# Row numbers of a neighbour search: added by a second product, or written into PSUM by ScalarE ahead of one product

## The chip, the cores and the metric

The kernel runs on one core of a Trainium2 chip. The metric is the device time of one execution in microseconds (us). A run is timed three times and the median is given. A separate execution is recorded by the profiler.

The engines are called by the profile's names: PE (TensorE), DVE (VectorE), ACT (ScalarE), POOL (GpSimd), SP (SyncE). Each works through its own queue in order. The matrix products write into PSUM[...].

## The reference

There are 4096 nodes of 128 features and an adjacency matrix of 4096 x 4096 integers, of which about one in 128 is 1. Cut to what matters:

```python
# layer 0: attention over the neighbours, 8 heads
Wh  = einsum('nd,hde->hne', nodes, W)
e   = leaky_relu(f1[:, :, None] + f2[:, None, :], 0.2)      # f1 = Wh.a1, f2 = Wh.a2
att = softmax(where(adj > 0, e, -9e15), axis=-1)
h   = elu(einsum('hnm,hmd->hnd', att, Wh))
x   = layernorm(nodes + elu(cat(h) @ W1 + b1))
# layer 1: for each node three quantiles over its kept neighbours, feature by feature
keep  = mask & ~((rank + 1) % skip == 0)
svals = sort(where(keep[:, :, None], x[None], big), axis=1)
agg   = mean of svals at ceil(q * n_keep) - 1, q in (0.25, 0.5, 0.75)
out   = (0.5 * agg + 0.5 * x) @ W.T + b + x
```

The kernel never forms the dense arrays: it finds each node's list of neighbours, at most 64, and gathers their rows.

## The kernel before, in words

**Three blocks.** The 32 tiles of 128 nodes are treated in blocks of 6, 10 and 16 (`BLOCKS`). For each block there is a *search* for the lists and then *attention*. The search of block 0 runs alone, beside the setup of the node rows (`node_rows`). Afterwards the attention of block 0 runs beside the search of the 10 tiles, and the attention of the 10 tiles beside the search of the 16. The prediction calls these two stretches block 0 and block 1. The attention of the last 16 tiles runs beside the making of layer 1's lists. Then comes the sort of layer 1, mostly on DVE.

**The search** (`neighbours`, L627). `load` (L634) brings half a tile of the adjacency matrix in a DMA of 1 MB, issued from ACT's queue; `sign` (L641) turns it into bfloat16 marks 0 or 1 (sgn) on ACT, sums them into cnt and issues the next load. A half tile has four chunks of 512 columns. For each chunk two products into one PSUM bank form keys: L684 multiplies the marks by 8192, and L687 adds a number that falls with the column (4096 minus the column), from two rows of `parts`. Thus a neighbour's key is over 8192 and tells its column. `eights` (L649) takes the eight largest of each 128 columns, four maxima a chunk (L651); `best` (L653) takes the eight largest that are left of the tile before (L656) and blanks them (L658). After eight chunks a tile is done; after up to four tiles `complete_records` writes them as records. The keys have two banks (pool kp), so the product of one chunk waits for the maxima of two chunks before. One chunk with its best is a *piece* of the generator, and the search yields after each.

**A step of attention** (`step`, L371). `fetch_rows` (L912) queues a tile's gathers on POOL, one indirect DMA for each slot of the list (L219), into tiles G of 16 slots. There are six G. `attend` (L938) works on the tile fetched one step earlier: the scores z (DVE, then an exponential on ACT, L959), their sums den on PE (L967) into the bank `small`, the reciprocals rden (DVE), spread by PE into rz (L983), multiplied into z (L994), laid out as wide (L1002), and then the weighted sums y on PE (L1015), one product for each slot with its G as weights. Only when these are done is a G free for the gathers of a later tile. The step's second half is done in the next step beside the next tile's first half: y is copied by ACT to yT (named late, L1028), PE multiplies with W into hT (L1034), ACT and DVE form the elu hv (L1040, L1042, L1043), PE multiplies with W1 into o (L1046), in the bank `small` too, and `finish_x1` makes the layer-0 row: v (L1069), ve, and rstd (L1081), scattered by POOL (L228).

**The order.** Within a step both generators are advanced in turn, and pieces of the search are put between them by count (`quota`). All of PE, DVE, ACT and POOL keep the order in which the program is written out (`manual_schedule`); only SP's is left to a scheduler. At the end of a block the search is finished, `rank_by_count` orders the block's nodes by list length, and POOL scatters the records among the last tile's gathers; SP reads them back as R and narrow.

**PSUM banks:** two for keys, one `small`, one rz, two y, two hT.

Of the kernel before, what the change touches and what calls it, by code (L numbers as in the profile page):

```python
# [9 lines left out]
F32 = mybir.dt.float32  # L10
BF16 = mybir.dt.bfloat16
I32 = mybir.dt.int32
AF = mybir.ActivationFunctionType
ALU = mybir.AluOpType
AX = mybir.AxisListType
PSUM = bass.MemoryType.PSUM
# [3 lines left out]
P = 128  # L20
N = 4096
D = 128
H = 8
# [6 lines left out]
L = 64  # L30
# [2 lines left out]
MARK = 8192.0  # L33
ROUNDS = L // 8
GROUP = 4
STEPS = 24
KEEP_MIN = 6.0
FMAX = 30.0
# [197 lines left out]
def iota(nc, dst, pattern, base=0, cm=0):  # L236
    nc.gpsimd.iota(  # L237
        dst, pattern=pattern, base=base, channel_multiplier=cm, allow_small_or_imprecise_dtypes=True
    )
# [3 lines left out]
def kernel(  # L243
# [15 lines left out]
    nc = tc.nc  # L259

    dram = ctx.enter_context(tc.tile_pool(name="dram", bufs=1, space=DRAM))
    xt_d = dram.tile([N + P, XW], F32, name="xt_d")
# [7 lines left out]
    ident = const.tile([P, P], F32, name="ident")  # L270
# [5 lines left out]
    pidx = const.tile([P, 1], F32, name="pidx")  # L276
    jp1 = const.tile([P, L], F32, name="jp1")
    vecs = const.tile([P, 4, D], F32, name="vecs")
    W_sb = const.tile([P, H, D], F32, name="W_sb")
    W1_sb = const.tile([P, H, D], F32, name="W1_sb")  # L280
    wa = const.tile([P, 2 * H], F32, name="wa")
    WlT = const.tile([P, D], F32, name="WlT")
    total = const.tile([1, 1], I32, name="total")
    bad = const.tile([P, 5, NT], F32, name="bad")
# [4 lines left out]
    rec = rp.tile([P, NT, REC], F32, name="rec")  # L289
    num = rp.tile([P, NT], F32, name="num")  # L290
    oneb = rp.tile([P, P], BF16, name="oneb")
    before = rp.tile([P, P], BF16, name="before")
    adjp = tc.alloc_tile_pool(name="adjp", bufs=2, side="right")
    cp = tc.alloc_tile_pool(name="cnt", bufs=2, side="right")
    kp = tc.alloc_tile_pool(name="key_ps", bufs=2, space=PSUM)
    parts = [adjp.tile([64, n], BF16, name=f"parts{n}", bufs=1) for n in (N // 8, 7 * N // 8)]
    markb = adjp.tile([P, P], BF16, name="markb", bufs=1)
    rowi = adjp.tile([P, P], F32, name="rowi", bufs=1)

    def search(t0, n):  # L300
        return neighbours(
            tc, adjp, cp, kp, rec, num, adj, t0, n, parts, markb, oneb, bad, jp1, pidx
        )

    with tc.tile_pool(name="setup", bufs=1) as sp, tc.tile_pool(
        name="setup_ps", bufs=2, space=PSUM
    ) as pp, tc.manual_schedule(engines=ORDERED):

        for v in parts:
            nc.vector.memset(v, 0.0)  # L310
        nc.vector.memset(oneb, 1.0)
        for v, base in zip(parts, (N, N - N // 8)):
            n = v.shape[1] // 64
            iota(nc, v[0:1, :], [[-64, n], [0, 64]], base=base)
            iota(nc, v[32:33, :], [[0, n], [-1, 64]])
        nc.vector.tensor_scalar(markb, ident, MARK, None, ALU.mult)
        iota(nc, pidx, [[0, 1]], cm=1)
        iota(nc, jp1, [[1, L]], base=1)
        nc.gpsimd.iota(
            rec.bitcast(I32)[:, :, R_OWN], pattern=[[P, NT]], base=0, channel_multiplier=1  # L320
        )
        iota(nc, rowi, [[1, P]])
        rows = node_rows(tc, sp, pp, rec, x, W, W_sb, a1, a2, Wl, wa, WlT, ident, bad, xt_d)
        for i, _ in enumerate(search(0, BLOCKS[0])):
            if i > 0:
                next(rows, None)
        for _ in rows:
            pass
        nc.vector.tensor_scalar(before, rowi, pidx, None, ALU.is_gt)
        nc.sync.dma_start(W1_sb, W1.rearrange("(h e) o -> e h o", e=P))  # L330
        for i, v in enumerate((b1, gamma, beta, bl)):
            nc.sync.dma_start(vecs[:, i, :], v.partition_broadcast(P))
        for i, big in enumerate((-BIG, BIG)):
            fill = sp.tile([P, D], F32, name=f"fill{i}")
            nc.gpsimd.memset(fill, big)
            nc.sync.dma_start(x1_d[N + i * P : N + (i + 1) * P, :], fill)
    attp = tc.alloc_tile_pool(name="att", bufs=2, reuse_waits="tile")
    pp = tc.alloc_tile_pool(name="att_ps", bufs=1, space=PSUM)
# [3 lines left out]

    weigh, store, tail = [], [], []
    consts = {}
    consts["small"] = pp.tile([P, 512], F32, name="small")

    narrow = {
        w: attp.tile([P, 32 // w, NARROW[w]], F32, name=f"narrow{w}", bufs=1) for w in NARROW
# [62 lines left out]
    t0 = 0  # L411
    with tc.manual_schedule(engines=ORDERED):
# [5 lines left out]
        for w in (32, 16, 8, 4):  # L418
            k = P // w
            v = const.tile([P, k], F32, name=f"v{w}")  # L420
# [7 lines left out]
        for w in (32, 16, 8, 4):  # L428
            k = P // w // 4
            v = const.tile([4, k, P], F32, name=f"vT{w}")  # L430
# [5 lines left out]
            W_sb=W_sb, W1_sb=W1_sb, vecs=vecs, eps_t=eps_t, ident=ident, own=own, ownT=ownT  # L436
        )
        for b, n in enumerate(BLOCKS):
            last = b == len(BLOCKS) - 1
            if last:  # L440
# [5 lines left out]
                cp = tc.alloc_tile_pool(name="cnt_all", bufs=2, side="right", reuse_waits="tile")  # L446
# [51 lines left out]
    with tc.tile_pool(name="sort", bufs=2) as sp, tc.tile_pool(name="fin", bufs=3) as fp, tc.tile_pool(  # L498
        name="fin_ps", bufs=2, space=PSUM
# [124 lines left out]
    return ROUNDS * (n + 1) + 3 * len(groups_of(n))  # L624


def neighbours(tc, adjp, cp, kp, rec, num, adj, t0, n, parts, markb, oneb, bad, jp1, pidx):  # L627


    nc = tc.nc  # L630
    half = N // 2
    loads, signs, firsts = [], [], []

    def load():  # L634
        if todo:
            t, i, cnt = todo.pop(0)
            adj_t = adjp.tile([P, half], I32, name="adj_t", bufs=3)
            nc.scalar.dma_start(adj_t, adj[ts(t, P), ts(i, half)])
            loads.append((t, i, cnt, adj_t))

    def sign():  # L641
        if loads:
            t, i, cnt, adj_t = loads.pop(0)
            sgn = adjp.tile([P, half], BF16, name="sgn", bufs=2)
            nc.scalar.activation(sgn, adj_t, AF.Sign, accum_out=cnt[:, i : i + 1])  # L645
            signs.append(sgn)
            load()

    def eights(key, first, c0):  # L649
        for c in range(512 // CW):  # L650
            nc.vector.max(first[:, ts(c0 // CW + c, 8)], key[:, ts(c, CW)])  # L651

    def best(first, t, r):  # L653

        top, rest = rec[:, t, ts(r, 8)], first[:, 8 * r :]
        nc.vector.max(top, rest)  # L656
        if r < ROUNDS - 1:
            nc.vector.match_replace(rest, top, rest, 0.0)  # L658

    todo, counts = [], {}  # L660
    for t in range(t0, t0 + n):
        cnt = adjp.tile([P, 2], F32, name="cnt", bufs=20)
        todo += [(t, 0, cnt), (t, 1, cnt)]
        counts[t] = cnt
    for _ in range(3):
        load()
    sign()
    late = None
    start = t0
    for t in range(t0, t0 + n + 1):  # L670

        if t < t0 + n:
            first = adjp.tile([P, NCH * 8], F32, name="first")
            firsts.append(first)
        for r in range(ROUNDS):
            done = late
            late = None
            if t < t0 + n:
                b = r % (ROUNDS // 2)
                if b == 0:  # L680
                    sgn = signs.pop(0)

                key = kp.tile([P, 512], F32, name="key")
                nc.tensor.matmul(  # L684
                    key, lhsT=markb, rhs=sgn[:, ts(b, 512)], start=True, stop=False
                )
                nc.tensor.matmul(  # L687
                    key, lhsT=oneb[0:64, :], rhs=parts[1][:, ts(r - 1, 512)] if r else parts[0], start=False, stop=True
                )
                late = (key, first, r * 512)  # L690
                if b == 0:
                    sign()
            if done:
                eights(*done)
            if t > t0:
                best(firsts[-2 if t < t0 + n else -1], t - 1, r)
            yield
        if t > t0:
            u = t - 1
            cnt = counts[u]  # L700
            nc.vector.tensor_tensor(num[:, u : u + 1], cnt[:, 0:1], cnt[:, 1:2], ALU.add)
            nc.vector.tensor_scalar(rec[:, u, 0:L], rec[:, u, 0:L], -MARK, 0.0, ALU.add, ALU.max)
            if t - t0 in groups_of(n):
                yield from complete_records(tc, cp, rec, num, bad, jp1, pidx, start, t - start)
                start = t
# [232 lines left out]
def attend(tc, ap, pp, fetched, consts):  # L938


    nc = tc.nc
    R, mine, parts = fetched
# [16 lines left out]
    nc.scalar.activation(zs, zs, AF.Exp)  # L959
    yield  # L960

    small = consts["small"]
    den = small[:, 0 : 32 * H]
    for i, (w, g0, runs, f1v) in enumerate(parts):
        k = P // w
        for r in range(k // 4):
            nc.tensor.matmul(  # L967
                den[0:4, :].rearrange("p (g r h) -> p r g h", r=k // 4, h=H)[:, r, g0:],
                lhsT=own[w][:, ts(r, 4)],
                rhs=z[:, layer[i] : layer[i] + w - g0, :],  # L970
                start=(i == 0 and r == 0),
                stop=(i == len(parts) - 1),
                skip_group_check=True,
# [2 lines left out]
    rden = ap.tile([4, 32 * H], F32, name="rden", bufs=1)  # L976
    nc.vector.tensor_scalar(rden, den[0:4, :], TINY, None, ALU.max)
    nc.vector.reciprocal(rden, rden)  # L978
    rz = pp.tile([P, L * H], F32, name="rz")
    for i, (w, g0, runs, f1v) in enumerate(parts):  # L980
        k = P // w
        for r in range(k // 4):
            nc.tensor.matmul(  # L983
                rz[:, layer[i] * H : (layer[i] + w - g0) * H],
                lhsT=ownT[w][:, r, :],
                rhs=rden.rearrange("p (g r h) -> p r g h", r=k // 4, h=H)[:, r, g0:],
                start=(i == 0 and r == 0),
                stop=(r == k // 4 - 1),
                skip_group_check=True,
# [51 lines left out]
    yield  # L1041
    nc.vector.tensor_scalar(hf, hf, 1.0, -1.0, ALU.min, ALU.add)  # L1042
    nc.vector.tensor_tensor(hf, hT, hf, ALU.max)  # L1043
    o = small[:, 32 * H : 32 * H + D]
    for h in range(H):
        nc.tensor.matmul(  # L1046
            o, lhsT=hv[:, h, :], rhs=consts["W1_sb"][:, h, :], start=(h == 0), stop=(h == H - 1)
# [453 lines left out]
```

## Time and profile before

| | |
|---|---|
| median of 3 runs | 3558.73 us (3556.36 to 3559.92) |
| the profiled execution's own time | 3561.78 us |
| its span, first to last instruction | 3560.0 us |
| PE busy | 1257.6 us (35%), 5323 products |
| DVE busy | 2700.2 us (76%) |
| ACT busy | 403.2 us (11%), 579 instructions |
| POOL busy | 2510.0 us (71%) |
| key products L684 and L687 | 256 each, 588 and 580 ns in the mean |
| gathers of the attention, L219 into G | 1124, 974 ns in the mean |
| granted clock of PE, mean | 0.562 |

A row of the profile names the line and engine, then what is written and what is read (out<-in), the count, the busy time and the mean of one. A wait names the instruction that ended it. Where the engine named had long been done, it was another. The busy time of products is modelled from a pipelined engine, so the distance from one start to the next says more than the length of one. The share of an engine over the whole span is a mean over stages that are bound by different things.

### The profile page before, as it was taken

How to read it: one execution, taken by the hardware profiler on the slowest of the kernel's cores; microseconds unless marked ns; L12 is line 12 of the kernel's file. 1: busy time of each engine (PE TensorE's matmuls, PEld its weight loads, DVE VectorE, ACT ScalarE, POOL GpSimd, SP SyncE). 2: the span in 40 equal slices, each digit the busy share in tenths (PEclk: the TensorE clock that was granted, in tenths of full speed). 3: DMA queues.
4: the chain of work that ended last, by engine and by line, in shares of the span. 5: the costliest groups of instructions: out<-in, count | busy, mean ns of one | idle time of the engine just before them, and what ended most of it. 6: DMA issues, size and time to landing. Idle time of an engine off the chain costs nothing. (4 is left out here: it accounts for less than half of the span.)

```text
span 3560.0 us, 22296 instructions
## 1 busy us (share of the span) xinstructions
PE 1257.6 (35%) x5323; PEld 949.8 (27%) x5323; DVE 2700.2 (76%) x7015; ACT 403.2 (11%) x579; POOL 2510.0 (71%) x2341
## 2 busy tenths in 40 slices
PE   7377568878555454555620000000000000000101
PEld 2144545555455454454520000000000000000101
DVE  8787458877435222247538999999999999999998
ACT  3122122222111111111110000000000000000000
POOL 1475767657777777777747777788777688777771
PEclk9955556555556555555555555555555555555555
DMA  6442254432222222232211111111111111111110
GB/s 232 136 150 77 67 159 131 139 119 75 59 65 54 56 53 55 54 70 55 52 30 48 47 46 46 43 43 41 44 42 46 34 40 41 41 42 41 40 42 12
DMA packets 109132, 237.42 MB, mean 67 GB/s; under 512 B 46720, under 2 KB 63104, under 8 KB 100800
## 3 DMA queue, kind: packets, MB, share of 16 engines
q0 software_dynamic: 74368, 156.34, 17.6%
q10 hardware_dynamic: 14848, 70.85, 5.8%
q1 hardware_dynamic: 19776, 8.73, 1.2%
q8 instruction: 44, 0.72, 0.1%
q14 instruction: 96, 0.79, 0.1%
HBM read 224.60 MB, written 11.15 MB: 66 GB/s over the span
## 5 line engine op out<-in xcount | busy, mean ns | idle before, releaser
L219 POOL DMA_INDIRECT vals<-x_d,idx x1024 | 1219.8, 1191 | 315.7 <-issue 308.7
L219 POOL DMA_INDIRECT G<-xt_d,idx x1124 | 1094.5, 974 | 419.9 <-issue 330.8
L1228 DVE TENSOR_TENSOR work<-work 128x512 f32<-128x512 f32 (+7 forms) x1194 | 933.7, 811 | 0.6
L1247 PE MATMUL st_ps<-dg,goal 128*128 128x128 f32 x286 | 71.4, 427 | 1605.9 <-DVE goal L1228 1605.1
L1228 DVE TENSOR_TENSOR work<-work,work 128x512 f32<-128x512 f32 (+6 forms) x821 | 590.8, 741 | 0.5
L1015 PE MATMUL y<-wide,G 128*128 128x32 f32 (+3 forms) x2248 | 485.6, 394 | 29.0 <-DVE wide L1002 28.9
L1247 PEld LDWEIGHTS st_ps<-dg,goal 128*128 128x128 f32 x286 | 63.3, 322 | 1612.3 <-issue 1611.4
L1015 PEld LDWEIGHTS y<-wide,G 128*128 128x128 f32 x2248 | 463.5, 310 | 65.4 <-DVE wide L1002 31.8
L651 DVE MAX8 first<-key 128x8 f32<-128x128 f32 x1024 | 225.2, 282 | 109.0 <-PE key L687 108.6
L952 DVE TENSOR_TENSOR z<-G,f1x 128x128 f32<-128x128 f32 (+5 forms) x92 | 28.8, 327 | 307.7 <-DMA G<-xt_d,idx 302.3
L684 PE MATMUL key<-sgn,markb 128*128 128x512 bf16 x256 | 150.5, 588 | 131.8 <-DVE first L651 87.9
L1228 DVE TENSOR_TENSOR work<-vals 128x1536 f32<-128x1536 f32 (+7 forms) x96 | 133.4, 1404 | 47.9 <-DMA vals<-x_d,idx 47.5
L1199 DVE COPY junk<-still 128x1 f32<-128x1 f32 x1118 | 168.8, 151 | 0.0
L645 ACT ACTIVATE sgn<-adj_t 128x2048 bf16<-128x2048 int32 x64 | 122.1, 1907 | 333.8 <-PE key L684 277.9
L1046 PE MATMUL small<-W_sb,late 128*128 128x128 f32 x512 | 127.3, 434 | 88.3 <-DVE late L1043 88.3
L1246 ACT ACTIVATE dg<-ident,wt 128x128 f32<-128x128 f32 x143 | 47.5, 394 | 930.9 <-PE st_ps L1247 930.6
L967 PE MATMUL small<-z,own 128*4 128x32 f32 (+6 forms) x438 | 49.3, 279 | 285.4 <-ACT z L959 285.4
L687 PE MATMUL key<-parts,oneb 64*128 64x512 bf16 x256 | 148.4, 580 | 0.5 <-POOL parts L237 0.5
L1046 PEld LDWEIGHTS small<-W_sb,late 128*128 128x128 f32 x512 | 112.8, 327 | 102.6 <-DVE late L1043 98.9
L983 PE MATMUL rz<-rden,ownT 4*128 4x32 f32 (+6 forms) x438 | 96.6, 383 | 78.6 <-DVE rden L978 63.7
L1034 PE MATMUL hT<-late,W_sb 128*128 128x128 f32 x512 | 110.2, 383 | 35.4 <-ACT late L1028 35.4
L228 POOL DMA_INDIRECT out_dram<-o,own_i x32 | 44.7, 1398 | 105.9 <-ACT o L1273 83.6
(184 smaller groups left out, 1784.4 us busy)
## 6 DMA issues: line engine op xcount, KB each, us to landing
adj_t<-in_adj_dram ACTq DMA_DIRECT2D x64, 1024.0 KB
G<-xt_d,idx POOLq DMA_INDIRECT x1124
vals<-x_d,idx POOLq DMA_INDIRECT x1024
R<-rec_d SPq DMA_DIRECT2D x128, 26.2 KB
xt_d<-rec SPq DMA_DIRECT2D x4, 544.0 KB
rec<-in_x_dram ACTq DMA_DIRECT2D x4, 512.0 KB
narrow<-rec_d SPq DMA_DIRECT2D x68, 5.2 KB
a_b<-in_L_gnn_a_dram ACTq DMA_DIRECT2D x2, 512.0 KB
```

Of the source, the lines that this page charges most:

```text
L219: nc.gpsimd.indirect_dma_start(out=dst, out_offset=None, in_=rows, in_offset=bass.IndirectOffsetOnAxis(ap=idx, axis=0),)
L645: nc.scalar.activation(sgn, adj_t, AF.Sign, accum_out=cnt[:, i : i + 1])
L651: nc.vector.max(first[:, ts(c0 // CW + c, 8)], key[:, ts(c, CW)])
L684: nc.tensor.matmul(key, lhsT=markb, rhs=sgn[:, ts(b, 512)], start=True, stop=False)
L687: nc.tensor.matmul(key, lhsT=oneb[0:64, :], rhs=parts[1][:, ts(r - 1, 512)] if r else parts[0], start=False, stop=True)
L983: nc.tensor.matmul(rz[:, layer[i] * H : (layer[i] + w - g0) * H], lhsT=ownT[w][:, r, :], rhs=rden.rearrange("p (g r h) -> p r g h", r=k // ...
L1015: nc.tensor.matmul(yf[:, ts(g, c)], lhsT=G[:, col + j - a, 0:D], rhs=pf[:, ts(j, c)], start=(i == 0 and g % (w // 2) == w // 2 - 1), stop= ...
L1034: nc.tensor.matmul(hT[:, ts(h, P)], lhsT=consts["W_sb"][:, h, :], rhs=yT[:, h, :], start=True, stop=True)
L1046: nc.tensor.matmul(o, lhsT=hv[:, h, :], rhs=consts["W1_sb"][:, h, :], start=(h == 0), stop=(h == H - 1))
L1199: nc.vector.tensor_copy(junk, late["still"])
L1228: nc.vector.tensor_tensor(slots_of(dst, (j, c, s, m), size), slots_of(a, (i, c, s, m), size), slots_of(b, (i + d, c, s, m), size), op,)
L1247: nc.tensor.matmul(st_ps[:, u, :], lhsT=goal[:, (j * k + u) * D : (j * k + u + 1) * D], rhs=dg, start=(j == 0), stop=False,)
```

## The change

ACT writes a chunk's row numbers into the PSUM bank with one instruction, an Identity of the fixed tile `rows` (0 to -511) plus a bias for each chunk (`base`); PE's one product then adds the marks to what lies there. These writes are called seeds here. The keys have three banks; two seeds are written at the start of a search and each further one two chunks ahead. For each of the three banks an opening product is issued first in each search. The sums den and the output o have no bank of their own any more: den lies in rz, o in hT.

```diff
+KEYS = 3
-    kp = tc.alloc_tile_pool(name="key_ps", bufs=2, space=PSUM)
-    parts = [adjp.tile([64, n], BF16, name=f"parts{n}", bufs=1) for n in (N // 8, 7 * N // 8)]
+    kp = tc.alloc_tile_pool(name="key_ps", bufs=3, space=PSUM)
+    rows = adjp.tile([P, 512], F32, name="rows", bufs=1)
+    base = adjp.tile([P, ROUNDS], F32, name="base", bufs=1)
...
-        for v in parts:
-            nc.vector.memset(v, 0.0)
         nc.vector.memset(oneb, 1.0)
-        for v, base in zip(parts, (N, N - N // 8)):
-            n = v.shape[1] // 64
-            iota(nc, v[0:1, :], [[-64, n], [0, 64]], base=base)
-            iota(nc, v[32:33, :], [[0, n], [-1, 64]])
+        iota(nc, rows, [[-1, 512]])
+        iota(nc, base, [[-512, ROUNDS]], base=N)
...
-    consts["small"] = pp.tile([P, 512], F32, name="small")
...
+    def seed(r):
+
+        key = kp.tile([P, 512], F32, name="key")
+        if len(opened) < KEYS:
+            nc.tensor.matmul(key, lhsT=markb, rhs=signs[0][:, 0:512], start=True, stop=True)
+            opened.append(key)
+        nc.scalar.activation(key, rows, AF.Identity, bias=base[:, r : r + 1])
+        seeded.append(key)
+
     for _ in range(3):
         load()
     sign()
+    opened, seeded = [], []
+    chunks = [r for _ in range(n) for r in range(ROUNDS)]
+    for _ in range(KEYS - 1):
+        seed(chunks.pop(0))
...
-                key = kp.tile([P, 512], F32, name="key")
+                key = seeded.pop(0)
                 nc.tensor.matmul(
-                    key, lhsT=markb, rhs=sgn[:, ts(b, 512)], start=True, stop=False
-                )
-                nc.tensor.matmul(
-                    key, lhsT=oneb[0:64, :], rhs=parts[1][:, ts(r - 1, 512)] if r else parts[0], start=False, stop=True
+                    key,
+                    lhsT=markb,
+                    rhs=sgn[:, ts(b, 512)],
+                    start=False,
+                    stop=True,
+                    skip_group_check=True,
                 )
...
             if done:
                 eights(*done)
+            if chunks:
+                seed(chunks.pop(0))
             if t > t0:
                 best(firsts[-2 if t < t0 + n else -1], t - 1, r)
...
-    small = consts["small"]
-    den = small[:, 0 : 32 * H]
+    rz = pp.tile([P, L * H], F32, name="rz")
+    den = rz[:, 0 : 32 * H]
...
-    rz = pp.tile([P, L * H], F32, name="rz")
...
-    o = small[:, 32 * H : 32 * H + D]
+    o = hT[:, 0:D]
```

More of the change, by code (lines that the diff above doesn't have):

```diff
@@ L301, in search @@
         return neighbours(
-            tc, adjp, cp, kp, rec, num, adj, t0, n, parts, markb, oneb, bad, jp1, pidx
+            tc, adjp, cp, kp, rec, num, adj, t0, n, rows, base, markb, bad, jp1, pidx
         )
@@ L322 @@
         iota(nc, rowi, [[1, P]])
-        rows = node_rows(tc, sp, pp, rec, x, W, W_sb, a1, a2, Wl, wa, WlT, ident, bad, xt_d)
+        own_rows = node_rows(tc, sp, pp, rec, x, W, W_sb, a1, a2, Wl, wa, WlT, ident, bad, xt_d)
         for i, _ in enumerate(search(0, BLOCKS[0])):
             if i > 0:
-                next(rows, None)
-        for _ in rows:
+                next(own_rows, None)
+        for _ in own_rows:
             pass
@@ L624, in pieces_of, with neighbours @@
     return ROUNDS * (n + 1) + 3 * len(groups_of(n))
-def neighbours(tc, adjp, cp, kp, rec, num, adj, t0, n, parts, markb, oneb, bad, jp1, pidx):
+def neighbours(tc, adjp, cp, kp, rec, num, adj, t0, n, rows, base, markb, bad, jp1, pidx):
     nc = tc.nc
```

## The prediction

> **What bounds the kernel now.** I read the tenths by slice first, then each queue's waits, then single stretches of the timeline. The first view shows two halves.
>
> ```profile
> PE   7377568878555454555620000000000000000101
> DVE  8787458877435222247538999999999999999998
> POOL 1475767657777777777747777788777688777771
> ```
>
> From slice 22 (1900 us) DVE is full: it sorts, the change touches nothing there, and what comes earlier only moves its start. Before that no engine is full, so a queue must be carrying the time. It is POOL's: each gather stands 1.25 us after the last (0.94 busy, 0.30 issue) from 137.7 us to 1770 us, and between them there are only these gaps over 4 us. Columns: start, duration, engine, line, operation; in brackets the idle time before it and what ended it.
>
> ```profile
> 321.66 0.94 POOL L219 DMA_INDIRECT G<-xt_d,idx  x1 [22.25 <-PE y L1015]
> 462.18 0.97 POOL L228 DMA_INDIRECT x_d<-x_t,mine  x1 [7.36 <-DVE f1b L898]
> 502.78 0.94 POOL L219 DMA_INDIRECT G<-xt_d,idx  x1 [6.89 <-PE y L1015]
> 696.89 1.04 POOL L219 DMA_INDIRECT G<-xt_d,idx  x1 [8.02 <-PE y L1015]
> 752.93 0.96 POOL L219 DMA_INDIRECT G<-xt_d,idx  x1 [29.97 <-PE y L1015]
> 854.58 0.97 POOL L219 DMA_INDIRECT G<-xt_d,idx  x1 [5.22 <-PE y L1015]
> ```
>
> Five of the six wait for the y products of an earlier tile to free a G buffer: 22.3 + 6.9 + 8.0 + 30.0 + 5.2 = **72 us**. From 854 us on POOL runs unbroken to 1770 us, with the sort behind it, so a microsecond taken off these gaps should reach the end whole, and 72 us is the most they can give. The records of the next block, which POOL must scatter at 427 and 927 us, are ranked by 388 and 919 us, so they do not hold it.
>
> Why is y late? First DVE's waits from 470 to 895 us (total, times, longest), then PE's timeline while POOL stands still before 321.66:
>
> ```profile
> DVE first L651 <- PE key L687: 72.5, 44, 4.8
> ```
>
> ```profile
> 312.25 0.60 PE L687 MATMUL key<-parts,oneb 64*128 64x512 bf16 x1
> 312.78 1.91 PE L1015 MATMUL y<-wide,G 128*128 128x32 f32 x8
> 314.51 0.61 PE L684 MATMUL key<-sgn,markb 128*128 128x512 bf16 x1
> 315.06 0.60 PE L687 MATMUL key<-parts,oneb 64*128 64x512 bf16 x1
> 315.59 0.61 PE L684 MATMUL key<-sgn,markb 128*128 128x512 bf16 x1
> 316.13 0.61 PE L687 MATMUL key<-parts,oneb 64*128 64x512 bf16 x1
> 316.67 1.91 PE L1015 MATMUL y<-wide,G 128*128 128x32 f32 x8
> 318.40 0.61 PE L684 MATMUL key<-sgn,markb 128*128 128x512 bf16 x1
> ```
>
> A chunk's two key products and four columns of y take 2.8 us in turn (315.59 to 318.40), back to back: here PE is the bound, and DVE, which needs about 1.7 to 2.0 us for the chunk (0.89 for four maxima, 0.35 to 0.43 for a best, about 0.5 for a replace), waits for it. In the first search it is otherwise: DVE is busy 92.3 of 97 us (10 to 107 us) and waits only 1.8 us for keys.
>
> **What the Trainium skill says.** "ScalarE: Activation LUTs", section "What ACT_TABLE_LOAD costs", prices an ACTIVATE with a pointer bias at 280 ns + 0.833 ns an element: 0.71 us for 512, an estimate. The trace agrees with the form: rstd (one element, pointer bias) 294 ns, sgn (2048 elements, no pointer) 1907 ns against 186 + 1706. The same page, "Table sets: the hidden batching unit", says that identity is in every set, so a seed between Exp and Sqrt needs no table; the trace has copies (L1028) in that place without a load. "PSUM — Partial Sum Buffer", "The four PSUM rules": ScalarE's writes leave the accumulate bits alone, and a product without the first flag adds where they are set. That is what the three opening products are for; nothing in the trace shows it. Its section "Engine vs sequencer instructions" calls ScalarE's queue strict FIFO; the trace shows sgn held 29.4 us at the head of ACT.
>
> **The change, part by part.**
>
> (1) PE loses 256 products L687. They follow their partner by 0.54 us and delay what follows by 0.54 us: 139 us of PE in all. The order of the two compiled programs says 265 key products remain, nine of them openers, and the attention's products keep their places. In the first search (48 chunks) DVE covers it: at most its 1.8 us. In an attention step the y stretch holds about 8 chunks in which PE is the bound: 8 x 0.54 = **4.3 us a step**. Block 0: three steps end before the gap at 321.66, 13 us off 22.3.
>
> Block 1: steps of about 48 us (464 to 897 us in nine), so the four gaps end in steps 1, 5, 6 and 8. Without gaps POOL would arrive at 495.9, 682.0, 708.0 and 804.5. The releases move from 502.8, 696.9, 752.9 and 854.6 to 498.5, 675.4, 727.1 and 820.2. POOL is then late by 2.6, 0, 19.1 and 15.7; the largest counts, 19 instead of the 50 of now: **31 us**. Together 44 us. What ends last then is POOL's own pitch of 1.25 us, and in step 6 still y.
>
> (2) ACT gains 256 seeds of 128x512. No row of before writes a key bank from ACT, so I bound one: xT takes 0.264 us for 128 elements and sgn 1.907 for 2048, 0.857 ns an element, so 0.59 us without a pointer; rstd's 0.294 and 511 more elements give 0.73. I take the page's 0.71, 182 us. ACT is busy 114 of 426 us in block 1; its 128 chunks add 91. Cover: ACT's idle time. Behind a waiting seed stand sgn with its adj load, the z, hT and ve exponentials and the y copy; PE, and DVE behind it, wait for them.
>
> (3) New waits: a key product waits for its seed, a seed for eights of three chunks before, where the product itself waited for two before. Seeds stand two chunks ahead, about 4 us at DVE's pace; the longest thing that can stand before one without waiting is sgn, 1.91 + 0.19, or the y copy with a table load, 1.88 + 1.28. That is under 4, so I cost it at nothing. Without that slack each late key costs DVE directly. Adj loads stay directly behind their sgn, sgn now behind up to four seeds (2.8 us) of an 8 us half tile. The exception is the start of block 1, where ACT is held at adj loads to 461.4 and 466.8 us: two seeds and an opener, 2 x 0.71 + 0.54 = 2 us **loss**.
>
> (4) Three banks for two: PE may run one chunk further ahead. PE waited 76 us for DVE's eights in blocks 0 and 1, 32 of it at a block's start. I take nothing: DVE is the later one there.
>
> (5) den in rz and o in hT. The den products wait for the last tile's z multiplication (L994), which PE already awaited for its y; o waits for DVE's reading of hT, which it already does through hv. The next hT waits for v (L1069) of the step before. Nothing in each case, covered by that order; gone, it costs up to a step's tail, some 3 us.
>
> (6) Setup. POOL loses four IOTAs of 8.0 us and gains two; 128x64 to 128x128 is 192 to 239 ns, so about 0.52 us for rows, 0.2 for base. DVE loses 1.8 us of memset while it idles. nodeq's wait (7.0 us, to 10.34) goes; the opener, seed and product that follow sgn at 8.0 make the first key about 10.2, and the third seed stands behind the second sgn. Within 1 us either way: 0. SP's queue is as before.
>
> Sum: -13 - 31 + 2 = -42 us. The profiled execution took 3561.8 (span 3560.0), 3.1 above the median; the difference is taken off the median: 3558.7 - 42 = **3517**.
>
> **Rivals.** *Full cover*: more than the y stretches shrink (DVE's 104 us of key waits in both blocks say it can), and all 72 go: 3487. Against it: POOL's longest gap, 30 us in step 6, needs 7.5 us a step. *DVE takes over*: DVE is busy 325 of 426 us in block 1, its waits turn into waits for o, rz and narrow, and y comes only half a microsecond earlier a step. Block 0 gives 1.5, block 1 4 (the last release at 850.6), the start takes 2: 3555. *ACT becomes a link in PE's chain*: every key waits for DVE, then ACT, and ACT itself stands waiting for z, v or y. It decides from the point at which a product waits for its seed over 0.54 us on average, more than was removed. With a net 3 us more a step, block 0 loses 9; in block 1 the last release moves to 878.6, 74 us late instead of 50: 33 us slower, 3592. For it: from 340 to 895 us ACT waited 107 us for v and 76 us for y. Against it: the two chunks of lead. *That it does not do what it says*: the program's order shows seeds and single products, so I give that nothing.
>
> **Numbers.** Main case 0.57, full cover 0.20, DVE takes over 0.08, ACT a link 0.15. 0.2% (7 us) is about what a measurement of this kernel can tell. The first two are faster (0.77), the third the same (0.08; its 3555 lies inside), the fourth slower (0.15). The range goes from full cover with 2 us of the first search, 3485, to 3560, which leaves out most of the slower case.
>
> **What would show it.** Right: L687 gone, seeds near 0.71 us, y stretches at 2.3 us a chunk, POOL's gaps near 9 and 19 us, DVE's key waits in block 1 under 40 us, the first sort gather about 42 us before 1818. Wrong: key products waiting for ACT by tens of us, POOL's gaps for y above 72 us, or gaps gone and the sort no earlier.

## The result, and the profile after

| | before | after |
|---|---|---|
| median | 3557.62 us (4 runs beside those of after) | 3519.09 us (3518.15 to 3520.08) |
| the profiled execution, its span | 3561.78, 3560.0 us | 3519.76, 3518.0 us |
| PE busy, products | 1257.6 us, 5323 | 1104.5 us, 5076 |
| ACT busy, instructions | 403.2 us, 579 | 566.4 us, 835 |

The ratio is 0.9892 (0.9880 to 0.9904): by the medians 38 us faster. The two profiled spans differ by 42.0 us, since the profiled execution of before, at 3561.78, was 4 us above its median.

The tenths by slice of the kernel after:

```profile
PE   4256565677266355456610001000000000001101
DVE  7788469888153122257448999999999999999998
POOL 0376767767777777777567777787776788777771
```

The form is that of before: no engine is full ahead of the sort, then DVE is. The digits of PE are mostly lower ahead of it, and the sort begins earlier. So POOL's queue is read next, its timeline from the first gather of the attention to the first gather of the sort. Columns as before: start, duration, engine, line, operation; in brackets the idle time and what ended it.

```profile
145.14 0.97 POOL L220 DMA_INDIRECT G<-xt_d,idx  x1 [5.12 <-DVE f1b L912]
317.43 0.94 POOL L220 DMA_INDIRECT G<-xt_d,idx  x1 [8.73 <-PE y L1028]
453.73 0.97 POOL L229 DMA_INDIRECT x_d<-x_t,mine  x1 [5.57 <-DMA x_d<-x_t,mine]
491.90 0.94 POOL L220 DMA_INDIRECT G<-xt_d,idx  x1 [4.14 <-PE y L1028]
715.03 0.97 POOL L220 DMA_INDIRECT G<-xt_d,idx  x1 [11.86 <-PE y L1028]
1776.44 0.98 POOL L220 DMA_INDIRECT vals<-x_d,idx  x1 [2.40 <-ACT halfid L499]
```

Three gaps for y are left of five: 8.73 + 4.14 + 11.86 = 24.7 us, where there were 72.4. That is 47.6 us less. The scatter's wait fell by 1.8 (7.36 to 5.57). Against that the first gather starts at 145.14 instead of 137.69, 7.45 us **later**. -47.6 - 1.8 + 7.45 = -42.0. The first gather of the sort moved from 1818.31 to 1776.44, by 41.9, and the span by 42.0. So POOL's queue accounts for the whole difference, gains and loss.

The reason for the shorter gaps is in PE's timeline ahead of 317.43, kernel after:

```profile
314.99 0.61 PE L694 MATMUL key<-sgn,markb 128*128 128x512 bf16 x1
315.40 1.75 PE L1028 MATMUL y<-wide,G 128*128 128x32 f32 x8
316.97 1.09 PE L694 MATMUL key<-sgn,markb 128*128 128x512 bf16 x2
317.85 1.75 PE L1028 MATMUL y<-wide,G 128*128 128x32 f32 x8
319.66 0.59 PE L694 MATMUL key<-sgn,markb 128*128 128x512 bf16 x1
```

Eight products of y with one key product now take 1.98 us (314.99 to 316.97), where with two they took 2.8. DVE's waits for keys in block 1 (430 to 865 us; total, times, longest) show it from the other side. In before the same stretch has 66.8 us in 41 waits.

```profile
DVE first L648 <- PE key L694: 32.1, 15, 5.2
```

What the seeds cost stands in the page's groups of the kernel after (busy, mean ns of one, then idle before and what ended most of it):

```profile
L668 ACT ACTIVATE key<-rows,base 128x512 f32<-128x512 f32 x256 | 174.5, 688 | 303.5 <-DVE first L648 245.4
L694 PE MATMUL key<-sgn,markb 128*128 128x512 bf16 x256 | 140.3, 574 | 141.5 <-ACT key L668 140.7
```

A seed takes 688 ns. It waits for DVE's maxima, as one wants: ACT is early. PE does wait 140.7 us for seeds, but most of this is the wait for DVE under another name, since a seed itself waits for its bank (128 x 512 float32 of PSUM in the row above): in block 1, PE waited 27.9 us for maxima before and 33.5 for seeds after. In the first 110 us, where the start is late, it was 12.1 before and 45.4 after.

The 7.45 us at the start are in ACT's timeline of the kernel after. An ACTq row is the issue of a DMA.

```profile
6.02 1.91 ACT L642 ACTIVATE sgn<-adj_t 128x2048 bf16<-128x2048 int32 x1 [2.56 <-DMA adj_t<-in_adj_dram]
7.83 0.19 ACT L642 ACTIVATION_READ_ACCUMULATOR sgn<-adj_t 128x1 f32 x1
13.02 0.36 ACTq L635 DMA_DIRECT2D adj_t<-in_adj_dram  x1
13.48 1.30 ACT L668 ACTIVATE key<-rows,base 128x512 f32<-128x512 f32 x2 [5.46 <-DMA vecs<-in_L_gnn_gamma_dram]
```

The first sgn is done at 8.0. Behind it in ACT's queue stands the issue of the fourth load of adj, and it waits until 13.0 us for a DMA of SP's queue that brings the small vectors (`vecs`). The first two seeds stand behind it. The first maxima begin at 14.85; in before they began at 10.42. There the fourth load was issued at 7.98, and the keys needed nothing of ACT but sgn.

### The profile page after: what moved, and what is told of

Its sections match the earlier page's. It is cut to its first block, busy times and chain, and to the rows that moved or that the text cites. A ratio compares the mean times of both kernels' runs of the same rounds, so it can differ in the third digit from the quotient of the medians.

```text
span 3518.0 us, 22186 instructions
## 1 busy us (share of the span) xinstructions
PE 1104.5 (31%) x5076; PEld 936.0 (27%) x5076; DVE 2694.2 (77%) x7013; ACT 566.4 (16%) x835; POOL 2502.2 (71%) x2339
## 3 DMA queue, kind: packets, MB, share of 16 engines
q1 hardware_dynamic: 19776, 8.73, 1.1%
## 5 line engine op out<-in xcount | busy, mean ns | idle before, releaser
L1028 PE MATMUL y<-wide,G 128*128 128x32 f32 (+3 forms) x2248 | 470.9, 387 | 35.6 <-DVE wide L1015 35.4
L668 ACT ACTIVATE key<-rows,base 128x512 f32<-128x512 f32 x256 | 174.5, 688 | 303.5 <-DVE first L648 245.4
L694 PE MATMUL key<-sgn,markb 128*128 128x512 bf16 x256 | 140.3, 574 | 141.5 <-ACT key L668 140.7
L1059 PE MATMUL hT<-W_sb,late 128*128 128x128 f32 x512 | 126.2, 431 | 98.7 <-DVE late L1056 98.7
L981 PE MATMUL rz<-z,own 128*4 128x32 f32 (+6 forms) x438 | 51.9, 289 | 298.0 <-ACT z L973 297.7
L1059 PEld LDWEIGHTS hT<-W_sb,late 128*128 128x128 f32 x512 | 114.1, 328 | 115.0 <-DVE late L1056 113.5
L642 ACT ACTIVATE sgn<-adj_t 128x2048 bf16<-128x2048 int32 x64 | 121.4, 1897 | 38.3 <-DMA narrow<-rec_d 28.8
```

Source lines behind the costliest of these rows:

```text
L668: nc.scalar.activation(key, rows, AF.Identity, bias=base[:, r : r + 1])
L694: nc.tensor.matmul(key, lhsT=markb, rhs=sgn[:, ts(b, 512)], start=False, stop=True, skip_group_check=True,)
L1028: nc.tensor.matmul(yf[:, ts(g, c)], lhsT=G[:, col + j - a, 0:D], rhs=pf[:, ts(j, c)], start=(i == 0 and g % (w // 2) == w // 2 - 1), stop= ...
L1059: nc.tensor.matmul(o, lhsT=hv[:, h, :], rhs=consts["W1_sb"][:, h, :], start=(h == 0), stop=(h == H - 1))
```

## The experiments

All times are medians beside runs of the kernel before: 3556.9 us for the first four, 3556.5 for the second four. Three columns are read from each trace.

| kernel | us | ratio to before | first gather | gaps for y | sort's first gather |
|---|---|---|---|---|---|
| before | 3557.6 | | 137.7 | 72.4 | 1818.3 |
| after | 3519.1 | 0.9892 (0.9880 to 0.9904) | 145.1 | 24.7 | 1776.4 |
| two_products | 3568.1 | 1.0030 (1.0019 to 1.0042) | 148.3 | 70.5 | 1825.7 |
| three_banks | 3557.2 | 0.9997 (0.9988 to 1.0006) | 137.2 | 66.4 | 1814.5 |
| seed_twice | 3547.1 | 0.9974 (0.9963 to 0.9984) | 164.0 | 32.2 | 1803.9 |
| start_order | 3516.0 | 0.9882 (0.9866 to 0.9899) | 144.3 | 18.3 | 1772.0 |
| fine_gathers | 3540.1 | 0.9949 (0.9934 to 0.9965) | 138.3 | 29.6 | 1798.9 |
| vecs_on_act | 3517.2 | 0.9887 (0.9872 to 0.9903) | 140.2 | 23.3 | 1769.7 |
| two_key_banks | 3540.1 | 0.9951 (0.9936 to 0.9967) | 150.9 | 38.1 | 1796.5 |
| start_and_fine | 3495.3 | 0.9829 (0.9816 to 0.9842) | 141.5 | 0 | 1750.8 |

### two_products: the time of the second product put back

The kernel after with a second product for each chunk, which adds zero.

```diff
                     start=False,
+                    stop=False,
+                    skip_group_check=True,
+                )
+                nc.tensor.matmul(
+                    key,
+                    lhsT=zerob[0:64, :],
+                    rhs=sgn[0:64, ts(b, 512)],
...
```

> The kernel after, with a second product put back into each chunk's group: 64 rows of zeros by the marks, accumulated, so the keys are the same. Seeds, three banks and shared banks stay. Theory (the gain is the 0.54 us of PE per chunk that no longer delays y): PE's y stretches go back to about 2.8 us a chunk, POOL's gaps for y from 25 us back to 65 to 80, and the time to 3519 + 48 = about 3565 us (3552 to 3575), over the kernel before, because the later start of the first search (7 us) stays. Rival (the gain is the third bank or the seeds standing ahead, PE's time does not count): 3519 to 3525, gaps near 25.

It came to 3568.1. POOL's timeline of this kernel has the longest gaps of before again, nearly to the microsecond:

```profile
334.88 0.94 POOL L220 DMA_INDIRECT G<-xt_d,idx  x1 [25.07 <-PE y L1038]
761.32 0.97 POOL L220 DMA_INDIRECT G<-xt_d,idx  x1 [28.97 <-PE y L1038]
```

Gaps for y grow by 45.8 us over after and the first gather comes 3.1 later: 48.9 of the 49.7 us between the spans. Seeds, third bank and shared den and o are all still there. So the gain of the change is what the second product takes on PE, and nothing else in it pays by itself. The product that was put back has 64 rows of weights like L687; the last section shows what that adds. A second product with 128 rows was not tried.

### three_banks: the banks alone

The kernel before with the banks of after: three of keys, den in rz, o in hT.

```diff
-    kp = tc.alloc_tile_pool(name="key_ps", bufs=2, space=PSUM)
+    kp = tc.alloc_tile_pool(name="key_ps", bufs=3, space=PSUM)
-    den = small[:, 0 : 32 * H]
+    den = rz[:, 0 : 32 * H]
-    o = small[:, 32 * H : 32 * H + D]
+    o = hT[:, 0:D]
```

> The kernel before with only the banks of the change: three banks of keys, den in rz, o in hT; both products stay and there are no seeds. Theory (the second product's time on PE is what counts): 3557 us, within 5; POOL's gaps for y 65 to 75 us, DVE's key waits over 60 us in block 1. Rival (the third bank lets PE run ahead, and that is the gain): 3520 to 3535, gaps under 45. If sharing den and o cost something of its own, it shows here as slower than before: 3560 to 3575.

3557.2, no difference that can be measured. The third bank did what banks do: in block 1 PE waited 0.9 us for maxima instead of 27.9. It brought nothing, since where PE waits for DVE, DVE is the later one. Sharing rz and hT costs nothing that shows here either; the two were not tried apart.

### seed_twice: double the seeds' time on ACT

```diff
-        nc.scalar.activation(key, rows, AF.Identity, bias=base[:, r : r + 1])
+        for _ in range(2):
+            nc.scalar.activation(key, rows, AF.Identity, bias=base[:, r : r + 1])
```

> The kernel after with each seed written twice, so ACT has 256 x 0.69 us more. Theory (seeds stand two chunks ahead and ACT's idle time covers them in the blocks): in the first search ACT needs about 2.2 us a chunk with sgn and the row copies against DVE's 2.0, so about 10 us are lost there and at the start; in blocks 0 and 1 at most another 8: 3529 to 3540 us. Rival (ACT is a link in PE's chain for each chunk): 208 chunks x 0.69 = 143 us more, 3660 us.

3547.1, 28 us over after, above the range that was given. The size was missed in the first search, where POOL's first gather tells what was lost:

```profile
163.96 0.97 POOL L220 DMA_INDIRECT G<-xt_d,idx  x1 [5.11 <-DVE f1b L913]
345.31 0.94 POOL L220 DMA_INDIRECT G<-xt_d,idx  x1 [19.59 <-PE y L1029]
```

The first search lost 18.8 us over after; the gaps for y grew by only 7.5. In the first search a half tile of about 8 us holds four seeds and a sgn, 4 x 0.69 + 2.1 = 4.9 us; doubled it is 7.6, and ACT is nearly the bound: DVE's waits for keys up to 125 us grew from 15.8 to 31.8 us. In the blocks 143 us of added ACT time (208 seeds) cost 7.5 us. There the slack is real, as the lead of two chunks had promised.

### two_key_banks: the lead cut to one chunk

```diff
-KEYS = 3
+KEYS = 2
-    kp = tc.alloc_tile_pool(name="key_ps", bufs=3, space=PSUM)
+    kp = tc.alloc_tile_pool(name="key_ps", bufs=2, space=PSUM)
```

> The kernel after with two banks of keys in place of three: seeds stand one chunk ahead of their product instead of two, and one bank lies unused. Theory (the lead of two chunks is what keeps ACT off the chain): the lead falls to about 2 us, so a sgn (2.1 us) or a copy of y with its table load (3.2 us) in front of a seed makes the key late. DVE's waits for keys grow by 20 us or more in the first search and by as much over both blocks, the first gather comes at 150 us or later, 3530 to 3545. Rival (the third bank is not needed, since DVE is the later one): waits as with three, 3519 to 3523.

3540.1, in the range. POOL's timeline:

```profile
150.88 0.98 POOL L220 DMA_INDIRECT G<-xt_d,idx  x1 [5.11 <-DVE f1b L912]
328.25 0.95 POOL L220 DMA_INDIRECT G<-xt_d,idx  x1 [13.73 <-PE y L1028]
733.49 0.97 POOL L220 DMA_INDIRECT G<-xt_d,idx  x1 [19.01 <-PE y L1028]
```

The start loses 5.7 and the gaps 13.3 us, 19 of the 20.0 by which the sort's first gather moved. DVE's waits for keys after 110 us grew from 52.5 to 67.5; in the first search they grew by 5.3 only. At least 20 had been expected for each, so the range was met with smaller waits than were thought of. The third bank, worth nothing with two products, is worth 20 us here: about half of the gain hangs on it, because it is what lets ACT be two chunks early.

### start_order and vecs_on_act: the lost start

start_order issues the fourth load with the second sgn's, lets the third opening product read the first sgn, so that a seed doesn't stand behind a later sgn, and puts a half tile's next sgn behind the seed of its chunk.

```diff
-            load()
+            for _ in range(owed.pop() if owed else 1):
+                load()
...
+    owed = [2, 0]
     sign()
-    opened, seeded = [], []
+    opened, seeded, lead = [], [], signs[0]
...
-            nc.tensor.matmul(key, lhsT=markb, rhs=signs[0][:, 0:512], start=True, stop=True)
+            nc.tensor.matmul(key, lhsT=markb, rhs=lead[:, 0:512], start=True, stop=True)
...
-                if b == 0:
-                    sign()
...
+            if t < t0 + n and b == 0:
+                sign()
```

> The kernel after with another order at a search's start and at a half tile's first chunk: the load behind the first sgn is issued with the second one's, the third opening product reads the first sgn, and sgn stands behind the seed of its chunk. Theory (the first search starts 6.9 us later than before because two seeds stand behind an adj load that waits for another DMA, and the third behind a sgn): first maxima at about 10 us in place of 14.85, the first gather 4 to 6 us earlier than 145.1, the end with it: 3513 to 3516 us. Rival (the start's loss is caught up at the POOL queue's waits for y, or sgn behind the seed now delays later chunks): 3518 to 3524.

The first maxima began at 10.18, as wanted, but the first gather gained 0.85 us only. The wait had moved with the load. ACT's timeline of this kernel:

```profile
16.37 1.91 ACT L669 ACTIVATE key<-rows,base 128x512 f32<-128x512 f32 x3 [3.15 <-DMA vecs<-in_L_gnn_beta_dram]
```

A DMA of the same kind ends the idle time, now three seeds later. The median, 3516.0, is 3 us under that of after, at the edge of what was expected, though not by the start: in the profiled execution the gaps of the blocks are 18.3 against 24.7. The intervals of the two ratios overlap, and which edit shortened the gaps was not separated. Next, the partner of the wait was taken away instead: vecs_on_act is the kernel after with these DMAs on ACT's own queue. ACT's order puts them behind the first search, so they are issued at 95 us there, not in the first 6 us.

```diff
-        nc.sync.dma_start(W1_sb, W1.rearrange("(h e) o -> e h o", e=P))
+        nc.scalar.dma_start(W1_sb, W1.rearrange("(h e) o -> e h o", e=P))
...
-            nc.sync.dma_start(vecs[:, i, :], v.partition_broadcast(P))
+            nc.scalar.dma_start(vecs[:, i, :], v.partition_broadcast(P))
```

> The kernel after, with the DMAs of W1_sb and of the small vectors (vecs) issued from ACT's queue instead of SP's, nothing else. Theory (at the start, ACT's fourth load of adj stands 5.5 us for a DMA of SP's queue that brings vecs, and the first seeds stand behind it; that is most of the 7.4 us by which the first gather comes later than before): the first maxima begin at about 10.2 us instead of 14.85, the first gather moves from 145.1 to 140 or 141, and the time is 3513 to 3516. Rival (the ring of transfers is full at that time, and the load waits for whatever is in flight): first maxima at 13 us or later, 3518 to 3522.

The wait is gone. ACT's timeline of this kernel, then DVE's:

```profile
7.76 0.34 ACTq L635 DMA_DIRECT2D adj_t<-in_adj_dram  x1
8.47 1.30 ACT L668 ACTIVATE key<-rows,base 128x512 f32<-128x512 f32 x2 [0.74 <-PE key L666]
```

```profile
9.84 0.89 DVE L648 MAX8 first<-key 128x8 f32<-128x128 f32 x4 [6.34 <-PE key L694]
12.80 4.20 DVE L648 MAX8 first<-key 128x8 f32<-128x128 f32 x20 [2.07 <-PE key L694]
19.12 1.68 DVE L648 MAX8 first<-key 128x8 f32<-128x128 f32 x8 [2.11 <-PE key L694]
```

The load is issued at 7.76 instead of 13.02. Fewer transfers are in flight here, but room among them is not what the load had waited for: in before W1_sb and vecs are brought at the same time as in after, and the fourth load was issued at 7.98. The records of the three traces say what it was, since they carry the semaphores that an instruction waits for and signals. The DMAs of SP's and ACT's queues share eight of them. In after the fourth load waits for sgn and for the one that the transfer of gamma into vecs signals (number 104); in vecs_on_act it waits for sgn alone. So it does in before, where only the fifth and later loads have such a wait: the fifth was issued at 16.56, with nothing but a sgn behind it. The first gather comes at 140.2, 4.95 us earlier, and the span is 3511.2. The median, 3517.2, lies above the range that was expected, and the ratio's interval overlaps that of after. The trace shows the cause and its 5 us; the times alone would not. The other 2.5 us of the start are near the two waits of 2.07 and 2.11, where a seed stands behind the second and third sgn.

### fine_gathers: fewer gaps with PE's work unchanged

The kernel before with tiles G of 8 slots.

```diff
-    G, col = None, 16
+    G, col = None, 8
...
-            if col == 16:
-                G, col = ap.tile([P, 16, XW], F32, name="G", bufs=6), 0
+            if col == 8:
+                G, col = ap.tile([P, 8, XW], F32, name="G", bufs=12), 0
```

> The kernel before, with two product per chunk as it was, and its six tiles G of 16 slots cut into twelve of 8 slots: the same bytes, the same gathers, but half a tile is free for the next gathers as soon as its 8 products of y are done. Theory (POOL's gaps for y carry the time one for one; PE's pace only sets how long they are): POOL's y gaps fall from 72 us to 40 to 50 with PE's work unchanged, the first sort gather comes earlier by the same amount, and the time is 3525 to 3540. Rival (the gaps go with PE's work as a whole, and buffers only move them): gaps stay within 8 us of 72 or something else is late in their place, 3550 to 3560.

The time, 3540.1, is at the upper edge of the range. The gaps fell further than expected, by 42.8 us to 29.6, but the sort's first gather moved by 19.5 only. POOL's timeline shows what took the rest:

```profile
680.66 0.94 POOL L219 DMA_INDIRECT G<-xt_d,idx  x1 [8.35 <-PE y L1015]
734.51 0.94 POOL L219 DMA_INDIRECT G<-xt_d,idx  x1 [17.50 <-PE y L1015]
835.08 0.94 POOL L219 DMA_INDIRECT G<-xt_d,idx  x1 [3.70 <-PE y L1015]
904.32 0.98 POOL L228 DMA_INDIRECT rec_d<-rec,ranks  x1 [19.20 <-DVE ranks L827]
```

POOL arrives at the records of the next block at 885 and must wait 19.2 us for their ranks, which are ready at 904. (In before they are ready at 918.5, but POOL only comes at 927.) With 5.1 us of the same kind at the end of block 0 (5.40 there, where before has 0.30), that makes -42.8 + 19.2 + 5.1 = -18.5, against 19.5 measured. So a gap that goes counts one for one only until the search's end is the later one. In after the last ranks are made at 863.9 us instead of the 918.5 of before: its single product hastens the search as well as y, and POOL finds the ranks ready.

### start_and_fine: both, and the finer tiles

The kernel after with the edits of start_order, vecs_on_act, and tiles G of 8 slots, thirteen of them.

> The kernel after with three edits: the start's order of loads, signs and opening products as in start_order, the DMAs of W1_sb and vecs on ACT's queue, and tiles G of 8 slots, thirteen of them. Theory (what is left of y gaps, 24.7 us, and of the start, 7.4 us, adds up): y gaps at 0 to 8 us in all, first gather at 138 to 141 us, 3492 to 3505. Rival (once the gaps are this small the sort is held by something else in front of it, the scatter or the last records): 3508 to 3518.

3495.3, ratio 0.9829 (0.9816 to 0.9842): faster than both kernels. POOL's timeline has no gap for y at all; the first and the last that matter:

```profile
141.48 0.98 POOL L220 DMA_INDIRECT G<-xt_d,idx  x1 [5.11 <-DVE f1b L914]
1750.77 0.98 POOL L220 DMA_INDIRECT vals<-x_d,idx  x1 [2.64 <-ACT dg L1261]
```

The sort begins 25.7 us earlier than in after, of the 28.4 that gaps (24.7) and start (3.7) held. With finer tiles alone the ranks took back half; here they come at 857.1, and nothing takes their gain.

## Why the prediction was right, and where it was not

**What bounds the kernel: right.** POOL's gaps for y are the currency. two_products moves them back by 46 us and the time with them. The limit of this reading was that the records do not hold POOL, which the prediction drew from ranks ready at 388 and 919 for scatters at 427 and 927. The first of these scatters in fact starts at 406.6, still behind its ranks. fine_gathers shows that the records do hold POOL when only the gaps shrink.

**(1) The second product: right in mechanism; the size was met by two errors that partly cancel.** Predicted -13 and -31, measured -13.5 and -34.1. Against the first gather, the release of block 0's gap moved by 11.7 us (183.97 to 172.29), 3.9 a step where 4.3 was worked out; the rest of the 13.5 is that POOL arrived 1.8 later. In block 1 the gaps that are left are 4.1 and 11.9, 16 in sum, predicted 19. The term of 0.54 us a chunk was too small for PE itself: a key product is now followed after 0.40 to 0.43 us, not 0.54, and eight of y mostly take 1.57, not 1.73. That is 0.83 us a chunk in the y stretch, 1.98 where the prediction named 2.3. The steps got less than eight times that: 3.9 / 0.83 is 4.7 chunks a step, an estimate from these two figures, in which PE is the bound, not eight.

**(2) and (3) Seeds: right.** 0.71 us was taken, 0.688 measured; the price of the Trainium skill ("ScalarE: Activation LUTs", section "What ACT_TABLE_LOAD costs"), 0.706 for 512 elements as an estimate, is 3% high here. The cover of two chunks was named with its limit, and two_key_banks shows it: without it 20 us. **Start of block 1:** +2 was predicted for ACT held at loads. Seeds do stand behind them, but POOL's wait at the scatter fell by 1.8 instead of rising. Whether the 2 us were lost and hidden was not separated.

**(4) and (5) Banks: right** to the accuracy of the measurement, by three_banks for both together, with a reservation. "I take nothing" holds for the third bank with two products; with seeds it is the lead of item (3), counted there.

**(6) Setup: wrong.** "Within 1 us either way" was 7.45 us slower. The step that failed is the order in ACT's queue: the prediction had the opener, seed and product follow sgn at 8.0, without asking what stands between sgn and seed. It is the issue of a load, held until 13.0. The prediction asked what is queued behind held loads in block 1 and not here. It went by the order of the two programs and not by what each instruction waits for, where the fourth load's second semaphore is to be seen; and ACT's timeline of before shows a load held from 10.9 to 16.56, which was warning enough. The other part, seeds behind the second and third sgn, was named and not priced.

**The sum** -42 is met by the two spans to a tenth, and that is chance: the block gaps gave 3.6 us more than worked out, the block-1 start 3.8 more, and the start took 7.45, which cancels the two.

**Rivals.** *Full cover* needed all gaps gone: 24.7 are left. *DVE takes over*: its waits for keys in block 1 fell from 66.8 to 32.1 us and did not turn into others, which were 66.2 in sum and are 62.1. *ACT a link*: what this would cost begins to show in two_key_banks, 20 us slower than after, and in seed_twice, 28 us slower; both are still faster than before.

## What to carry to other kernels

Find the queue whose gaps add up to the time, and price a change by the gaps that it shortens; then look for what that queue meets next when it comes early, as the ranks here. Work given to an idle engine is free only with a lead: a third buffer that is worth nothing by itself was worth 20 us as the lead of the seeds. Before an instruction is put into a queue, look at what is issued ahead of it, DMA issues too, above all in the first microseconds, when every load is in flight.

## What the hardware showed that was not expected

- The issue of a DMA on ACT's queue waited 5 us for a DMA from SP's queue, of other data into another tile, only because both signal through one of eight semaphores; all of ACT stood behind it. Which DMA gets which semaphore moved with the change, though neither queue's first DMAs did: in before the fourth load signals the same semaphore as the first, whose sgn is done; in after a transfer of SP's has taken that one (into xt_d, issued at 6.07 instead of 12.72). A longer hold of the same kind stands at the start of block 1 in both kernels, 29.4 us before and 28.8 after: the second of three loads of adj shares its semaphore with a transfer into `narrow`, which SP issues only at 443.1 us (449.8 in before). ACT's timeline of after follows; whether these 28.8 us cost time was not tried.

```profile
444.90 1.79 ACTq L635 DMA_DIRECT2D adj_t<-in_adj_dram  x2
446.73 1.91 ACT L642 ACTIVATE sgn<-adj_t 128x2048 bf16<-128x2048 int32 x1 [28.78 <-DMA narrow<-rec_d]
```

- PE paced faster with less work, and not by its clock. Two windows of the y stretch ahead of the first gap (us, PE busy and count, granted clock, DMA share, GB/s), of before and then of after, have the same granted clock, 0.50:

```profile
315.00:318.00 3.00, 3.00 (x11) 0.50 0.01 3
```

```profile
315.00:317.00 2.00, 2.00 (x11) 0.50 0.00 0
```

A product of y follows the last after 0.213 us in both. The difference is in the loads of weights into PE (PEld). In before they start only with the product that needs them (L687 at 316.13, y at 316.67):

```profile
316.13 0.10 PEld L687 LDWEIGHTS <-oneb 64*128 64x128 bf16 x1 [0.44 <-issue]
316.67 1.78 PEld L1015 LDWEIGHTS y<-wide,G 128*128 128x128 f32 x8 [0.43 <-issue]
```

In after they start under the product before. The weights of y, whose first product comes at 315.40, are loaded from 314.99 on, with the key product:

```profile
314.78 0.29 PEld L694 LDWEIGHTS <-markb 128*128 128x128 bf16 x1
314.99 2.02 PEld L1028 LDWEIGHTS y<-wide,G 128*128 128x128 f32 x8
```

What goes with it is whether the shape of the weights stays the same. In the first 1820 us of before, among products that follow each other within 1 us, 93% of 3301 loads start more than 30 ns ahead of their product where both products have 128 rows and 128 columns of weights, and 85% of 405 where both have 4 rows. From 128 rows to 64 it is none of 255, and from 64 to 128 it is 2% of 198. So L687, with its 64 rows, cost PE its own 0.54 us and also about 0.13 in its partner (0.54 against 0.41) and 0.16 in the eight of y behind it (1.73 against 1.57). two_products, again with 64 rows, has 0.54 and 1.73 again. This is read from traces; no run changed the rows alone.
